# A slot-attention kernel: the key side in blocks of 64 tokens instead of 128

## The chip, the cores and the metric

The kernel runs on one core of a Trainium2 chip. The core has five engines that run side by side and wait for each other through semaphores: TensorE (PE, matrix products; PEld is its loading of weights), VectorE (DVE), ScalarE (ACT), GpSimd (POOL) and SyncE (SP, which here only starts transfers). TensorE writes its results into PSUM, which has eight banks of 128 partitions x 512 f32; DVE and ACT read them from there. The metric is the device time of one launch in microseconds, the lower the better.

## The reference

Four sequences of 512 tokens with 512 features go through one layer: a gated slot attention with 16 heads (keys of 64, values of 128, 64 slots), and a feed-forward part with rounded weights. The part that matters here is the recurrence of each head over time. In the notation of the reference:

```python
z = jax.lax.cumlogsumexp(s, axis=2)
g = jnp.exp(jnp.concatenate([z[:, :, :1], z[:, :, :-1]], axis=2) - z)
p = jnp.exp(s - z)
...
def step_k(hk, x):
    q_t, k_t, p_t, g_t = x
    hk = hk * g_t[:, :, None, :] + k_t[..., None] * p_t[:, :, None, :]
    return (hk, jnp.einsum('bhk,bhkm->bhm', q_t, hk))
_, okT = jax.lax.scan(step_k, hk0, (qT, kT, pT, gT))
pvT = jax.nn.softmax(okT, axis=-1)
```

With e = exp(s) and z turned into the running sum of e, the decay cancels: the score of token t for slot m is the sum over all tokens u up to t of (q_t . k_u) e_u[m], divided by the running sum of e[m] at t. That is a causal linear attention. It can be worked out in blocks of tokens: within a block by a masked product of queries and keys times e, and for all earlier blocks through a state, the sum of k_u e_u over their tokens (64 x 64 for each head). A second recurrence of the same form then carries the values; it stays as it is.

## The kernel before, in words

The attention is cut into 32 units, one for each pair of heads g (0 to 7) and sequence b (0 to 3). The order is g 0 to 7 for b 0 and 1 in turn, then the same for b 2 and 3. After the units comes the feed-forward part for the four sequences. The whole program is under a manual schedule: each engine runs its instructions in the order in which the code emits them, so the order of the calls in `attention` is the order of the work on every engine.

Two heads share a unit, each with 64 of the 128 partitions wherever a tile holds "slots" or "keys". A unit projects slots, keys and queries (`project`, L557), turns e and the keys so that tokens lie on partitions (`turn_e`, L697, `turn_k`, L702), projects the values (`project_v`, L570) and the gate (`gate_main`, L823, `gate_mixed`, L831), and takes the scores through a softmax to the values. The output of the unit before is finished in between: `turn_output` (L837: four transposes on PE, then a product on DVE at L842), `high_output` (L847, ACT), `split_output` (L850, DVE), `project_output` (L861), `add_output` (L882, which also starts a transfer from POOL's queue).

The key side, which is changed, uses blocks of 128 tokens, four to a sequence (NT = 4):

- `key_states` (L707) forms the three states that are needed after block 0, 1 and 2: `states` (L630) makes six f32 products of 128 tokens, 64 columns each, the two heads in the two column halves of the array, into one PSUM bank. `add_up` (L645) adds them up on DVE: one copy, two additions. POOL copies the sums into `sk_both` (L713), whose blocks are 128 x 128 with the two heads on the diagonal and zeros beside it, cleared once at the start (L136).
- `query_key` (L715) calls `diagonal_blocks` (L607): eight products of 64 x 128 with 128 columns, the heads in the two row halves of the array, into two banks of the pool "acc"; then two masking products on DVE (L626) with the triangle `tri`.
- `slot_scores` (L718) sums into one bank: three products of `sk_both` with the queries (128 x 128, L724), then eight of e with the masked blocks (128 x 64, heads in the column halves, L731). DVE multiplies the bank by the inverse running sum into okT (L739), and `softmax` (L741) starts by transposing okT on PE.

Where these stand differs with g. In units of even g the order is turn_e, turn_k, values(0), values(1), turn_output(0) and (1) each followed by its high_output, key_states, inverse, query_key, values(2), split_output(0), values(3). In units of odd g it is turn_e, turn_output(0), turn_k, turn_output(1), both high_outputs, query_key, key_states, both split_outputs, inverse. Then in both the gate, slot_scores, value_states, softmax and the output projection follow. For b of 2 and 3 DVE also rounds the feed-forward weights (`quantize`, L461) in between.

PSUM is shared out by hand: three banks are taken in turn by `bank` (L110), two belong to "acc", three to the projections ("proj"). A tile that takes a bank waits until the last reader of its previous tile is done. The banks in turn are used by the transposes, by the states of keys and values, and by the second call of `diagonal_blocks`:

```python
    def bank(name, n=None):
        if n is None:
            n = turn[0]
            turn[0] = (n + 1) % 3
        if n in held:
            held.pop(n)()
        return ps1.tile([P, 512], F32, tag=f"bank{n}", name=name)
```

SBUF tiles are shared by tags in the same way: "ok" holds the softmax, "sv" the value states, "kn" the turned keys and later okT, "a0" and "a1" the masked blocks of both sides.

Of the kernel before, what the change touches and what calls it, by code (L numbers as in the profile page):

```python
# [37 lines left out]
F32 = mybir.dt.float32  # L38
# [3 lines left out]
ALU = mybir.AluOpType  # L42
AX = mybir.AxisListType

P = 128
# [4 lines left out]
def kernel(  # L50
# [18 lines left out]
    nc = tc.nc  # L69

    B, T, D = x.shape
# [4 lines left out]
    NT = T // P  # L76
    KC = D // P
    HG = 2
    NG = H // HG
    HM = HG * M  # L80
# [6 lines left out]
    const = ctx.enter_context(tc.tile_pool(name="const", bufs=1))  # L87
    xpool = ctx.enter_context(tc.tile_pool(name="xpool", bufs=2))
    one = ctx.enter_context(tc.tile_pool(name="one", bufs=1))
# [3 lines left out]
    ps2 = ctx.enter_context(tc.tile_pool(name="ps2", bufs=2, space=bass.MemoryType.PSUM))  # L93
# [4 lines left out]
    turn = [0]  # L98
    held = {}
# [10 lines left out]
# [7 lines that stand above are left out]
# [5 lines left out]
    tri = const.tile([P, P], F32, tag="tri", name="tri")  # L122
# [10 lines left out]
    mhalf = const.tile([P, NH], F32, tag="mhalf", name="mhalf")  # L133
    nc.gpsimd.memset(mhalf, -0.5)

    sk_both = const.tile([P, NT - 1, HM], F32, tag="sk_both", name="sk_both")  # L136
    nc.gpsimd.memset(sk_both, 0.0)
    QMAX = 464.0

    NS = 2 * NFC + 1  # L140
# [29 lines left out]
    def other(count=None):  # L170
        for _ in range(count or pace[0]):
            if work:
                work.pop(0)[1]()
# [9 lines left out]
    def need(key):  # L183

        while any(name == key for name, _ in work):
            other(1)
# [4 lines left out]
    for g in range(NG):  # L191
# [3 lines left out]
        for nm in names:  # L195
            n = g if nm != "v" else 0 if g == 0 else (g + 1) // 2
# [96 lines left out]
    def next_step():  # L293
        if steps:
            steps.pop(0)()
# [310 lines left out]

    def diagonal_blocks(lT, rT, name):  # L607

        if name[0] == "a":
            pa = [ps2.tile([P, T], F32, tag="acc", name=f"ps_{name}_{h}") for h in range(HG)]  # L610
        else:
            pa = []
            for h in range(HG):
                if turn[0] in held:
                    turn[0] = (turn[0] + 1) % 3
                pa.append(bank(f"ps_{name}_{h}"))
        pa = [p.rearrange("p (n t) -> p n t", n=NT) for p in pa]
        for n in range(NT):
            cols = slice(n * P, (n + 1) * P)
            for h in range(HG):  # L620
                rows = slice(h * M, (h + 1) * M)
                nc.tensor.matmul(pa[h][:, n, :], lT[rows, cols], rT[rows, cols], start=True, stop=True)  # L622
        blocks = []
        for h in range(HG):
            a = one.tile([P, NT, P], F32, tag=f"a{h}", name=f"{name}_{h}")
            nc.vector.tensor_tensor(a, pa[h], tri.unsqueeze(1).to_broadcast([P, NT, P]), ALU.mult)  # L626
            blocks.append(a)
        return blocks

    def states(left, right, right0, width, name):  # L630


        pt = bank(name)[:, : (NT - 1) * width].rearrange("p (n w) -> p n w", w=width)
        for n in range(NT - 1):
            for h in range(HG):
                nc.tensor.matmul(
                    pt[h * M : (h + 1) * M, n, :],
                    left[:, n, h * M : (h + 1) * M],
                    right[:, n, right0 + h * width : right0 + (h + 1) * width],
                    start=True,  # L640
                    stop=True,
                )
        return pt

    def add_up(state, pt):  # L645

        nc.vector.tensor_copy(state[:, 0, :], pt[:, 0, :])
        for n in range(1, NT - 1):
            nc.vector.tensor_tensor(state[:, n, :], pt[:, n, :], state[:, n - 1, :], ALU.add)  # L649
# [3 lines left out]
    class Heads:  # L653
# [48 lines left out]
        def turn_k(self):  # L702
            pt = transpose_4(self.kT, f"ps_kn_{self.u}")
            self.kn = one.tile([P, NT, HM], F32, tag="kn", name=f"kn_{self.u}")
            nc.scalar.copy(self.kn, pt)

        def key_states(self):  # L707
            pt = states(self.kn, self.e, 0, M, f"ps_sk_{self.u}")
            self.sk = one.tile([P, NT - 1, M], F32, tag="sk", name=f"sk_{self.u}")
            add_up(self.sk, pt)  # L710
            for h in range(HG):
                rows = slice(h * M, (h + 1) * M)
                nc.gpsimd.tensor_copy(sk_both[rows, :, h * M : (h + 1) * M], self.sk[rows])  # L713

        def query_key(self):  # L715
            self.a = diagonal_blocks(self.kT, self.qT, f"a_{self.u}")

        def slot_scores(self):  # L718


            pok = ps2.tile([P, T], F32, tag="acc", name=f"ps_ok_{self.u}")
            for n in range(1, NT):
                cols = slice(n * P, (n + 1) * P)
                nc.tensor.matmul(  # L724
                    pok[:, cols], sk_both[:, n - 1, :], self.qT[:, cols],
                    start=(n == 1), stop=False,
                )
            for n in range(NT):
                for h in range(HG):
                    rows = slice(h * M, (h + 1) * M)  # L730
                    nc.tensor.matmul(  # L731
                        pok[rows, n * P : (n + 1) * P],
                        self.e[:, n, rows],
                        self.a[h][:, n, :],
                        start=False,
                        stop=(n == NT - 1),
                    )
            self.okT = one.tile([P, T], F32, tag="kn", name=f"okT_{self.u}")
            nc.vector.tensor_tensor(self.okT, pok, self.rzT, ALU.mult)  # L739

        def softmax(self):  # L741

# [147 lines left out]
    def first_unit():  # L890


        X = Heads(0, 0)

        parts = layernorm(0, 1, first=lambda: X.values(0))
        for nm in "skqv":
            load_matrix(nm, 0, True)
        for item in [item for item in work if item[0] in ("s_", "k_", "q_")]:
            work.remove(item)
            item[1]()  # L900
        X.values(1)
        for _ in range(5):
            piece()
        transposing = layernorm(1, 1)
        work.extend(parts())
        load_matrix("g", 0, True)
        other(2)
        X.slots()
        other(2)
        X.keys(X.running_sum)  # L910
        other(2)
        X.queries(None)
        X.turn_e()
        X.turn_k()
        other(2)
        X.values(2)
        other(2)
        X.key_states()
        X.inverse()
        X.values(3)  # L920
        fetch()
        fetch()
        load_matrix("o", 0, True)
        other(1)
        transposing()
        next_step()
        other(2)
        X.query_key()
        next_step()
        other(3)  # L930
        X.gate_main(0)
        X.slot_scores()
        X.value_states()
        next_step()
        X.softmax()
        X.softmax_exp()
        other(1)
        X.gate_main(1)
        X.slot_weights()
        next_step()  # L940
        X.gate_silu(0)
        X.gate_silu(1)
        exp_and_log()
        X.weight_slot()
        need("xs_1")
        X.softmax_sum()
        need("xs_0")
        piece()
        X.read_out()
        return X  # L950

    def attention(g, b, before, load, gated):
# [3 lines left out]
        X = Heads(g, b)  # L956
# [4 lines left out]
        def early_step():  # L961

            if not any(name.endswith("_m") for name, _ in work):
                next_step()

        need(f"xs_{b}")
        need("s")
        X.slots()
# [20 lines left out]
        if even:  # L989
            X.turn_k()  # L990
            next_step()
            if turned():
                other(1)
            need("v")
            X.values(0)
            if first or b > 1:
                other(1)
            X.values(1)
            before.turn_output(0)
            before.high_output(0)  # L1000
            before.turn_output(1)
            before.high_output(1)
            X.key_states()
            X.inverse()
            X.query_key()
            other()
            X.values(2)
            before.split_output(0)
            next_step()
            other()  # L1010
            X.values(3)
            other()
            next_step()
            before.split_output(1)
        else:
            before.turn_output(0)
            X.turn_k()
            before.turn_output(1)
            before.high_output(0)
            before.high_output(1)  # L1020
            X.query_key()
            X.key_states()
            if b > 1:
                early_step()
            before.split_output(0)
            before.split_output(1)
            X.inverse()
            if work and work[0][1] is scale_low:
                other(1)
            if work and work[0][0] == "o":  # L1030
                other()
# [153 lines left out]
    with tc.manual_schedule(engines=EVERY):  # L1185
# [83 lines left out]
        for b in range(B):  # L1269
            need(f"xs_{b}")  # L1270
            for c in range(NFC):
                if c > 1:
                    other(2)
                h = ffn_hidden(b, c)
# [74 lines left out]
```

## Time and profile before

| what | value |
|---|---|
| time, median of 3 runs | 1456.88 us (1455.47 to 1457.69) |
| span of the profiled execution | 1454.5 us (what lies around it isn't on the page; the median less the span is 2.4 us) |
| granted TensorE clock, mean | 0.999 |
| ps_sk, matmul passes (L636, N = 64) | x384, median 222 ns |
| ps_a (L622), ps_ok (L731), N = 128 | x512 each, median 272 and 273 ns |
| ps_ok (L724), N = 128 | x192, median 275 ns |
| masks of a on DVE (L626) | x64, median 680 ns |
| okT on DVE (L739) | x32, median 692 ns |
| sk copies on POOL (L713) | x64, mean 679 ns |

A matmul's duration in the trace runs from its start to its end, and the next ones start long before that: the distance between starts is what it costs the stream. The count of passes is twice the count of f32 matmuls in the code. In a timeline a line is a run of equal instructions: its start, the time from the first start to the last end, engine, line, operation, tiles, shape, count, and in brackets the idle time of the engine before it with what ended it. In the chain, pieces follow each other without overlap, so their lengths add up.

### The profile page before, as it was taken

How to read it: one execution, taken by the hardware profiler on the slowest of the kernel's cores; microseconds unless marked ns; L12 is line 12 of the kernel's file. 1: busy time of each engine (PE TensorE's matmuls, PEld its weight loads, DVE VectorE, ACT ScalarE, POOL GpSimd, SP SyncE). 2: the span in 40 equal slices, each digit the busy share in tenths (PEclk: the TensorE clock that was granted, in tenths of full speed). 3: DMA queues.
4: the chain of work that ended last, by engine and by line, in shares of the span. 5: the costliest groups of instructions: out<-in, count | busy, mean ns of one | idle time of the engine just before them, and what ended most of it. 6: DMA issues, size and time to landing. Idle time of an engine off the chain costs nothing.

```text
span 1454.5 us, 22772 instructions
## 1 busy us (share of the span) xinstructions
PE 1429.6 (98%) x8875; PEld 1178.9 (81%) x8875; DVE 1104.0 (76%) x1968; ACT 709.9 (49%) x1215; POOL 240.0 (16%) x271
## 2 busy tenths in 40 slices
PE   9999999999999999999999999999999999999998
PEld 4778888888888888888888888888888788888886
DVE  6888868976897689878888898898889863435333
ACT  4555555555665556554545554556445542222221
POOL 2012111211121122211211121111112111000000
PEclk9999999999999999999999999999999999999999
DMA  8274556565655474456546654666465562101000
GB/s 333 86 218 138 182 160 172 175 191 158 174 174 185 135 232 123 138 156 192 160 109 196 203 161 108 196 203 173 127 179 174 145 181 30 59 0 58 1 29 29
DMA packets 80859, 212.51 MB, mean 146 GB/s; under 512 B 6168, under 2 KB 35120, under 8 KB 75568
## 3 DMA queue, kind: packets, MB, share of 16 engines
q1 hardware_dynamic: 62224, 177.49, 33.1%
q0 software_dynamic: 18528, 33.58, 15.2%
q8 instruction: 70, 1.15, 0.3%
q14 instruction: 37, 0.30, 0.1%
HBM read 107.23 MB, written 108.00 MB: 148 GB/s over the span
## 4 chain that ended last, share of the span: by engine, by line
PE 89%; DVE 7%; ACT 2%; issue 1%; POOL 0%; DMA 0%; DVEq 0%; POOLq 0%
PE ps_o L869 8%; PE ps_g L528 8%; PE ps_v L587 7%; PE ps_fg L1097 6%; PE ps_fu L1097 6%; PE ps_ov L793 4%; PE ps_o_m L869 4%; PE ps_g_m L551 4%; PE ps_v_m L587 4%; PE ps_s L528 3%; PE ps_k L528 3%; PE ps_q L528 3%; PE ps_fd L1158 3%; PE ps_fe L1158 3%; PE ps_b L622 2%; PE ps_a L622 2%
## 5 line engine op out<-in xcount | busy, mean ns | idle before, releaser
L885 POOL DMA_DIRECT2D stream<-y x128 | 112.4, 884 | 476.3 <-DVE y L884 468.6
L869 PE MATMUL ps_o<-w_o,oT 128*128 128x512 f32 x512 | 145.2, 405 | 0.0
L528 PE MATMUL ps_g<-xs,w_g 128*128 128x512 f32 x496 | 125.2, 394 | 0.0
L587 PE MATMUL ps_v<-w_v,xs 128*128 128x512 f32 x480 | 122.3, 397 | 0.2 <-DVE qT L555 0.2
L1118 DVE SCALAR_TENSOR_TENSOR h<-ps_fu,scol,act 128x512 f32<-128x512 f32 x48 | 36.0, 750 | 111.5 <-PE ps_fu L1097 110.2
L879 ACT ACTIVATE y<-ps_o 128x512 f32<-128x512 f32 x128 | 76.5, 598 | 74.9 <-PE ps_o L869 74.9
L528 PEld LDWEIGHTS ps_g<-xs,w_g 128*128 128x128 f32 x496 | 91.7, 188 | 19.7
L869 PEld LDWEIGHTS ps_o<-w_o,oT 128*128 128x128 f32 x512 | 91.4, 188 | 17.4
L587 PEld LDWEIGHTS ps_v<-w_v,xs 128*128 128x128 f32 x480 | 87.7, 188 | 19.4 <-DVE qT L555 0.6
L713 POOL COPY sk_both<-sk 64x192 f32<-64x192 f32 x64 | 43.5, 679 | 343.4 <-DVE sk L649 341.5
L1097 PE MATMUL ps_fg<-xs,wf 128*128 128x512 f32 x384 | 95.6, 391 | 0.0
L884 DVE TENSOR_TENSOR y<-y,ps_o_m 128x512 f32<-128x512 f32 x128 | 87.2, 681 | 10.4 <-ACT y L879 9.8
L1097 PE MATMUL ps_fu<-xs,wf 128*128 128x512 f32 x384 | 94.8, 389 | 0.0
L595 ACT ACTIVATE v<-ps_v 128x512 f32<-128x512 f32 x60 | 35.9, 599 | 99.9 <-PE ps_v L587 99.9
L803 ACT ACTIVATE og<-ps_ov 128x512 f32<-128x512 f32 x64 | 38.1, 597 | 94.5 <-PE ps_ov L793 94.5
L1097 PEld LDWEIGHTS ps_fu<-xs,wf 128*128 128x128 f32 x384 | 72.1, 188 | 15.0
L1097 PEld LDWEIGHTS ps_fg<-xs,wf 128*128 128x128 f32 x384 | 71.6, 188 | 14.6
L869 PE MATMUL ps_o_m<-w_o,oT 128*128 128x512 f32 x256 | 79.4, 391 | 0.2 <-ACT y L879 0.2
L596 DVE TENSOR_TENSOR v<-v,ps_v_m 128x512 f32<-128x512 f32 x60 | 41.0, 684 | 48.6 <-PE ps_v_m L587 48.6
L1124 ACT CAST both<-h 128x512 fp32r<-128x512 f32 x48 | 29.8, 621 | 94.5 <-DVE h L1118 94.5
L1115 ACT ACTIVATE act<-ps_fg,scol 128x512 f32<-128x512 f32 x48 | 33.0, 688 | 87.7 <-PE ps_fg L1097 87.7
L533 ACT ACTIVATE sg<-ps_g 128x512 f32<-128x512 f32 x62 | 37.0, 596 | 71.4 <-PE ps_g L528 44.4
(171 smaller groups left out, 3327.0 us busy)
## 6 DMA issues: line engine op xcount, KB each, us to landing
stream<-y POOLq DMA_DIRECT2D x128, 256.0 KB, 6.3
split_v<-w_v SPq DMA_DIRECT2D x4, 3072.0 KB, 12.3
split_g<-w_g SPq DMA_DIRECT2D x8, 1536.0 KB, 7.6
split_o<-w_o SPq DMA_DIRECT2D x8, 1536.0 KB, 6.3
w_v<-split_v SPq DMA_DIRECT2D x4, 3072.0 KB, 16.3
w_g<-split_g SPq DMA_DIRECT2D x8, 1536.0 KB, 6.6
w_o<-split_o SPq DMA_DIRECT2D x8, 1536.0 KB, 9.5
rounded<-qw SPq DMA_DIRECT2D x36, 256.0 KB, 3.7
```

The costliest lines, as they stand in the source:

```text
L528: nc.tensor.matmul(self.p, products(self.nm, c, self.col0, i), xs[self.b][i][:, c, :], start=(i == 0 and c == 0), stop=(i == 1 and c == KC ...
L551: nc.tensor.matmul(self.m, products(self.nm, c, self.col0, 2), xs[self.b][2][:, c, :], start=(c == 0), stop=(c == KC - 1),)
L587: nc.tensor.matmul(dst, xs[b][i][:, c, n * P : (n + 1) * P], wt["v"][:, i, c * 2 * HV : (c + 1) * 2 * HV], start=(i == which[0] and c == 0 ...
L622: nc.tensor.matmul(pa[h][:, n, :], lT[rows, cols], rT[rows, cols], start=True, stop=True)
L713: nc.gpsimd.tensor_copy(sk_both[rows, :, h * M : (h + 1) * M], self.sk[rows])
L793: nc.tensor.matmul(po[h][:, n, :], self.bb[h][:, n, :], both_v[self.b][:, n, self.v0 + h * DV : self.v0 + (h + 1) * DV], start=False, stop ...
L869: nc.tensor.matmul(dst, self.oT[:, i, h, n * P : (n + 1) * P], wt["o"][:, i, h * D : (h + 1) * D], start=(i == which[0] and h == 0), stop= ...
L879: nc.scalar.mul(y, p, 1.0 + DELTA)
L884: nc.vector.tensor_tensor(y, y, m, ALU.subtract)
L885: nc.gpsimd.dma_start(stream[self.b][n * P : (n + 1) * P, :], y, accum_op=ALU.add)
L1097: nc.tensor.matmul(pp, w[:, c * P : (c + 1) * P], xs[b][k][:, c, :], start=(c == 0 and k == 0), stop=(c == KC - 1 and k == 1),)
L1158: nc.tensor.matmul(sums[n], parts[k][:, n * P : (n + 1) * P], fw[c][2], start=(c == 0 and k == 0), stop=(c == NFC - 1 and k == 1),)
```

## The change

Blocks of the key side become 64 tokens long, eight to a sequence (SB = 64). A block of 128 tokens now has two halves, "sub" 0 and 1.

- `key_states` makes 14 products of 64 x 64 with 64 columns: the half of the block picks the row half of the array, the head the column half. The two halves go to two banks taken in turn. ACT copies the first bank into a new tile "own" (tag "sv"), DVE adds the second bank to it and adds up over blocks (three operations), and POOL writes the sums into `sk_even` and, added to own, into `sk_odd` (six operations in all). `sk_odd` shares the tag "ok" with the softmax, so POOL clears it in every unit (`clear_odd`), at the unit's start.
- `query_key` makes 16 products of 64 x 64 with 64 columns: the head picks the row half, the half of the block the column half. The masks are 128 x 256 for each head.
- `slot_scores` sums into two banks of "acc", one for each half: 14 products of the seven states (128 x 64, 64 columns, head by head), and 16 of e with the masked blocks (64 x 64, 64 columns). okT is written by two DVE operations, one for each bank.
- In units of odd g key_states moves ahead of query_key.

```diff
-    sk_both = const.tile([P, NT - 1, HM], F32, tag="sk_both", name="sk_both")
-    nc.gpsimd.memset(sk_both, 0.0)
+    SB = P // 2
+    tri_sub = const.tile([P, SB], F32, tag="tri_sub", name="tri_sub")
+    for sub in range(2):
+        rows = slice(sub * SB, (sub + 1) * SB)
+        nc.gpsimd.tensor_copy(tri_sub[rows, :], tri[rows, rows])
+
+    sk_even = const.tile([P, NT - 1, HM], F32, tag="sk_even", name="sk_even")
+    nc.gpsimd.memset(sk_even, 0.0)
...
+        def clear_odd(self):
+
+            self.sk_odd = one.tile([P, NT, HM], F32, tag="ok", name=f"sk_odd_{self.u}")
+            nc.gpsimd.memset(self.sk_odd, 0.0)
+
         def key_states(self):
-            pt = states(self.kn, self.e, 0, M, f"ps_sk_{self.u}")
-            self.sk = one.tile([P, NT - 1, M], F32, tag="sk", name=f"sk_{self.u}")
-            add_up(self.sk, pt)
+
+            pts = [
+                bank(f"ps_sk_{self.u}_{sub}")[:, : NT * M].rearrange("p (n w) -> p n w", w=M)
+                for sub in range(2)
+            ]
+            for n in range(NT):
+                for sub in range(2):
+                    toks = slice(sub * SB, (sub + 1) * SB)
+                    for h in range(HG):
+                        if 2 * n + sub == 2 * NT - 1:
+                            continue
+                        cols = slice(h * M, (h + 1) * M)
+                        nc.tensor.matmul(
+                            pts[sub][cols, n, :], self.kn[toks, n, cols], self.e[toks, n, cols],
+                            start=True, stop=True,
+                        )
+            own = one.tile([P, NT, M], F32, tag="sv", name=f"sk_own_{self.u}")
+            nc.scalar.copy(own, pts[0])
+            sk = one.tile([P, NT - 1, M], F32, tag="sk", name=f"sk_{self.u}")
+            nc.vector.tensor_tensor(sk, pts[1][:, : NT - 1, :], own[:, : NT - 1, :], ALU.add)
+            for n in range(1, NT - 1):
+                nc.vector.tensor_tensor(sk[:, n, :], sk[:, n, :], sk[:, n - 1, :], ALU.add)
             for h in range(HG):
                 rows = slice(h * M, (h + 1) * M)
-                nc.gpsimd.tensor_copy(sk_both[rows, :, h * M : (h + 1) * M], self.sk[rows])
+                nc.gpsimd.tensor_copy(self.sk_odd[rows, 0, rows], own[rows, 0, :])
+            for h in range(HG):
+                rows = slice(h * M, (h + 1) * M)
+                nc.gpsimd.tensor_copy(sk_even[rows, :, rows], sk[rows])
+                nc.gpsimd.tensor_tensor(
+                    self.sk_odd[rows, 1:, rows], own[rows, 1:, :], sk[rows], ALU.add
+                )
 
         def query_key(self):
-            self.a = diagonal_blocks(self.kT, self.qT, f"a_{self.u}")
+
+            pa = [ps2.tile([P, T], F32, tag="acc", name=f"ps_a_{self.u}_{h}") for h in range(HG)]
+            pa = [p[:, : NT * SB].rearrange("p (n t) -> p n t", n=NT) for p in pa]
+            for n in range(NT):
+                for sub in range(2):
+                    c = slice((2 * n + sub) * SB, (2 * n + sub + 1) * SB)
+                    for h in range(HG):
+                        rows = slice(h * M, (h + 1) * M)
+                        nc.tensor.matmul(
+                            pa[h][sub * SB : (sub + 1) * SB, n, :], self.kT[rows, c], self.qT[rows, c],
+                            start=True, stop=True,
+                        )
+            self.a = []
+            for h in range(HG):
+                a = one.tile([P, NT, SB], F32, tag=f"a{h}", name=f"a_{self.u}_{h}")
+                nc.vector.tensor_tensor(
+                    a, pa[h], tri_sub.unsqueeze(1).to_broadcast([P, NT, SB]), ALU.mult
+                )
+                self.a.append(a)
 
         def slot_scores(self):
...
+            for c in range(1, 2 * NT):
+                n, sub = divmod(c, 2)
+                state = self.sk_odd[:, n, :] if sub else sk_even[:, n - 1, :]
+                for h in range(HG):
+                    cols = slice(h * M, (h + 1) * M)
+                    nc.tensor.matmul(
+                        pok[sub][cols, n, :], state[:, cols], self.qT[:, c * SB : (c + 1) * SB],
+                        start=(c <= 2), stop=False,
+                    )
             for n in range(NT):
-                for h in range(HG):
-                    rows = slice(h * M, (h + 1) * M)
-                    nc.tensor.matmul(
-                        pok[rows, n * P : (n + 1) * P],
-                        self.e[:, n, rows],
-                        self.a[h][:, n, :],
-                        start=False,
-                        stop=(n == NT - 1),
-                    )
+                for sub in range(2):
+                    toks = slice(sub * SB, (sub + 1) * SB)
+                    for h in range(HG):
+                        cols = slice(h * M, (h + 1) * M)
+                        nc.tensor.matmul(
+                            pok[sub][cols, n, :], self.e[toks, n, cols], self.a[h][toks, n, :],
+                            start=False, stop=(n == NT - 1),
+                        )
             self.okT = one.tile([P, T], F32, tag="kn", name=f"okT_{self.u}")
-            nc.vector.tensor_tensor(self.okT, pok, self.rzT, ALU.mult)
+            okT, rzT = (t.rearrange("p (n s t) -> p n s t", s=2, t=SB) for t in (self.okT, self.rzT))
+            for sub in range(2):
+                nc.vector.tensor_tensor(okT[:, :, sub, :], pok[sub], rzT[:, :, sub, :], ALU.mult)
...
             before.high_output(0)
             before.high_output(1)
+            X.key_states()
             X.query_key()
-            X.key_states()
```

`clear_odd` is called at the start of each unit, ahead of the projection of the slots.

More of the change, by code (lines that the diff above doesn't have):

```diff
@@ L607, in diagonal_blocks @@
     def diagonal_blocks(lT, rT, name):
[L609 to L612, printed above, removed]
-            for h in range(HG):
-                if turn[0] in held:
-                    turn[0] = (turn[0] + 1) % 3
-                pa.append(bank(f"ps_{name}_{h}"))
+        pa = []
+        for h in range(HG):
+            if turn[0] in held:
+                turn[0] = (turn[0] + 1) % 3
+            pa.append(bank(f"ps_{name}_{h}"))
         pa = [p.rearrange("p (n t) -> p n t", n=NT) for p in pa]
@@ L711, in key_states @@
             for h in range(HG):
                 rows = slice(h * M, (h + 1) * M)
-                nc.gpsimd.tensor_copy(sk_both[rows, :, h * M : (h + 1) * M], self.sk[rows])
-        def query_key(self):
-            self.a = diagonal_blocks(self.kT, self.qT, f"a_{self.u}")
-        def slot_scores(self):
[L721 to L726, printed above, removed]
-                )
-            for n in range(NT):
-                for h in range(HG):
-                    rows = slice(h * M, (h + 1) * M)
-                    nc.tensor.matmul(
-                        pok[rows, n * P : (n + 1) * P],
-                        self.e[:, n, rows],
-                        self.a[h][:, n, :],
-                        start=False,
-                        stop=(n == NT - 1),
-                    )
+                nc.gpsimd.tensor_copy(self.sk_odd[rows, 0, rows], own[rows, 0, :])
@@ new lines, in slot_scores @@
+        def slot_scores(self):
+            pok = [
+                ps2.tile([P, T], F32, tag="acc", name=f"ps_ok_{self.u}_{sub}") for sub in range(2)
+            ]
+            pok = [p[:, : NT * SB].rearrange("p (n t) -> p n t", n=NT) for p in pok]
+            for c in range(1, 2 * NT):
[7 more added lines that the diff above has]
+                    )
+            for n in range(NT):
+                for sub in range(2):
+                    toks = slice(sub * SB, (sub + 1) * SB)
+                    for h in range(HG):
+                        cols = slice(h * M, (h + 1) * M)
[3 more added lines that the diff above has]
+                        )
@@ L900, in first_unit @@
             item[1]()
+        X.clear_odd()
         X.values(1)
@@ L964, in early_step @@
                 next_step()
+        X.clear_odd()
         need(f"xs_{b}")
```

## The prediction

> **What bounds the kernel now.** I read the page first: busy times and the chain that ended last.
>
> ```profile
> PE 1429.6 (98%) x8875; PEld 1178.9 (81%) x8875; DVE 1104.0 (76%) x1968; ACT 709.9 (49%) x1215; POOL 240.0 (16%) x271
> PE 89%; DVE 7%; ACT 2%; issue 1%; POOL 0%; DMA 0%; DVEq 0%; POOLq 0%
> ```
>
> TensorE sets the end for 89% of the span, DVE for 7%. So an edit counts twice: what it takes from TensorE's stream, and what it does to DVE where TensorE waits for it. Second, the chain in order of time, through unit (0,2):
>
> ```profile
> 611.01 0.87 PE ps_oT L604 x8
> 611.88 0.50 PE ps_sk L636 x12
> 612.38 1.09 PE ps_a L622 x16
> 613.47 2.04 PE ps_v L587 x8
> ...
> 626.07 0.67 PE ps_ok L724 x6
> 626.74 1.05 PE ps_ok L731 x16
> 627.78 0.02 issue
> 627.81 0.70 DVE okT L739
> 628.51 0.04 issue
> 628.55 0.66 PE ps_okn L604 x4
> ```
>
> Each f32 matmul shows as two passes (6 matmuls of sk are x12). The touched work is 0.50 + 1.09 + 0.67 + 1.05 = 3.3 us of a unit, 106 us over 32 units; behind it TensorE stands until DVE has written okT. Third, the timelines of DVE and ACT, in even unit (2,2), then in odd unit (1,2):
>
> ```profile
> 756.86 1.40 DVE L842 SCALAR_TENSOR_TENSOR sg<-ps_oT,scol,sg 128x512 f32<-128x512 f32 x2
> 758.18 0.21 DVE L647 COPY sk<-ps_sk 128x64 f32<-128x64 f32 x1
> 757.64 1.29 ACT L848 ACTIVATE oT<-sg 128x512 fp32r<-128x512 f32 x2 [1.76 <-DVE sg L842]
> 771.47 0.69 DVE L739 TENSOR_TENSOR okT<-ps_ok,rzT 128x512 f32<-128x512 f32 x1 [0.57 <-PE ps_ok L731]
> ```
> ```profile
> 690.36 0.58 ACT L705 COPY kn<-ps_kn 128x512 f32<-128x512 f32 x1 [0.29 <-PE ps_kn L604]
> 690.71 1.16 PE L622 MATMUL ps_a<-qT,kT 64*128 64x128 f32 x16
> 693.11 0.21 DVE L647 COPY sk<-ps_sk 128x64 f32<-128x64 f32 x1
> 699.83 0.69 DVE L739 TENSOR_TENSOR okT<-ps_ok,rzT 128x512 f32<-128x512 f32 x1 [0.63 <-PE ps_ok L731]
> ```
>
> DVE is about 0.6 us early for okT. In most units it runs from sk to there without a gap, so a delay of DVE above 0.6 us near sk reaches TensorE.
>
> **Prices on TensorE.** From the matmul start times of the trace: sk starts two passes, one in each column half, every 0.058 us (64 columns); a and the e·a products of ok start two every 0.109 to 0.111 (128 columns). A change of tile shape adds 0.093 before the first pass; the first slot of 64 wide passes is 0.048 longer than the later ones.
>
> The unknown is a slot with four 64x64 tiles. One end is 0.058 (all four run together), the other 0.116 (two at a time, as seen). I take 0.058: near 558 us the two row halves of ps_b ran 23 ns out of step, each at its own 0.111, and ps_ov started in one half before ps_b's last pass in the other. Halves are thus fed independently.
> [...]
>
> **Key side, per unit.** Before: span of sk 0.347, change 0.152, a 0.890, change 0.202: 1.591 us from sk's start to the next group. After: sk is 14 matmuls, at most 8 slots a tile, 0.048 + 7 x 0.058 = 0.454; a follows in the same shape, 0.058 + 0.42 (0.406 and 0.014 for the tiles' stagger); change 0.151. Sum 1.083: **-0.508**. Then two new waits.
> Even g: sk now takes two banks, and of the three in turn the second is that of turn_output(0), which DVE's first L842 frees at 0.66 after sk's start in every even unit. Only the first pair of products goes ahead; sk ends 1.05 instead of 0.454 after its start: +0.60, net **+0.09**. Queued behind the waiting matmul: the rest of sk, a, values(2).
> Odd g: key_states moves ahead of query_key, so the copy of kn (ends at 690.94; a started at 690.71) is no longer covered by a's matmuls: +0.30, net **-0.21**.
>
> **Scores.** From the last gate matmul to okn it was 0.233 + 0.557 + 0.205 + 0.822 + 1.069 = 2.886. After: 0.320 (the shape changes here too), 14 state products, two at a time, 0.802; change 0.151; e·a 0.468. The last pass is 0.05 shorter, so okT could start 0.126 earlier. But okT is now two operations of 256: between 291 ns (128) and 692 (512) I get 0.425, with 0.08 overlap 0.77 instead of 0.69: +0.08. The change of shape into sv (0.146) hides under okT.
>
> **DVE, ACT, POOL.** The first DVE operation of sk waits for a new ACT copy "own", which is queued behind both L848. In (2,2) these end 1.98 after sk's start, own (256 columns: between 374 and 600 ns, say 0.44) at 2.44. DVE's sum starts at 2.49 and hands over at 3.28 (0.79 for three operations instead of 0.65); before it was 1.88: 1.40 late. The masks of a shrink from 2 x 0.61 to 2 x 0.345, -0.53: **0.87 late** from then on. Queued behind: inverse, split_output, the value and gate subtractions, okT. Odd g, by the same count from a's start (L848 ends at 1.52, own at 2.0, next 3.53 instead of 3.05): **0.48 late**.
> POOL has six operations where it had two copies of 0.68, and a memset (0.41 for 384 columns, some 0.55; POOL idles many us before it). A row for 64x192 additions is missing; between 0.68 and 1.28 (128x512). In odd g the chain ends 5.8 to 7.0 after a's start, scores begin at 7.0: hidden, just. Where POOL's copies ran beside DVE, L852 took 0.826 instead of 0.684: 0.14 for two copies. With four more operations I take 2 x 0.14, +0.3 on DVE; the ends are 0 (the copies beside other operations cost nothing) and 4 x 0.14, 0.56.
> [...]
>
> **Sum at okn.** TensorE offers okT -0.34 (odd) or -0.04 (even); DVE offers it at lateness minus idle minus 0.08; the later counts, plus 0.08.
> - Odd, 13 units with idle about 0.61: 0.78 - 0.69 = +0.09, so +0.17 each, 2.2. Units (1,1), (7,1) have no idle: +0.85 each, 1.7. (7,3) has a gap of 1.63: -0.26.
> - Even, b below 2: gaps of DVE swallow the 1.17; +0.04 x 7 = 0.3. b of 2 and 3: idle 0.57 twice gives +0.60, 0.83 three times +0.34, the rest +0.04: 2.3.
> - (0,0), without the two waits: -0.3.
>
> Together +5.9 us. The span 1454.5 + 5.9, and 2.4 around it (median 1456.88 less the span): **1462.8**. The feed-forward part (from 1180 us) is untouched.
>
> **Rivals.**
> 1. *Four tiles don't run four at a time*, so the change does not do what it says. [...] At 0.116: +1.13 and +1.43, 41 us: 1498. For it: no four tiles in this trace. Against: the independent halves. 0.24.
> 2. *Not slower: DVE's idle covers the late sum.* Place: the gap before okT. If lateness stays under some 0.3 in odd and 0.6 in even units (own faster, no POOL cost), TensorE's times count: 16 x (-0.26) + 16 x 0.04 = -3.5, 1453. If sk's second bank is also free at once, 15 x 0.6 = 9 more: 1444. For it: the 0.6 us gaps, and DVE loses 0.2 us of work a unit. Against: ACT's order is fixed, with L848 ahead of own. It decides from the point where okT still shows idle time before it in odd units. About 1449; 0.20.
> 3. *The forecast*: TensorE saves, and the bank, kn, own and POOL take it back. 0.56; own range 1453 to 1472.
>
> **From these.** Predicted 1463. Below 1450 lies about half of rival 2, above 1488 about a third of rival 1, so the range is 1450 to 1488. A measurement tells 0.2% (2.9 us) from no change. Faster than 1454: 0.17 of rival 2 and 0.08 of the forecast, 0.25. Within: 0.03 and 0.12, 0.15. Slower: 0.60.
>
> **What would show it.** Right: ps_a and the e·a products about 0.45 us each; a wait of sk for DVE's L842 in even units, for kn in odd ones; DVE idle over 1 us before sk's first operation, on ACT; no idle before okT in odd units. Wrong: ps_a still 0.9 us (rival 1); idle before okT (rival 2); TensorE waiting for POOL at the state products, which I count as hidden.

## The result, and the profile after

The changed kernel takes 1470.87 us (median of 4 runs, 1468.55 to 1473.83) against 1456.24 us before: a ratio of 1.0103, 95% interval 1.0091 to 1.0114. Slower, as forecast, and inside the range, but by 14.6 us where 6 were forecast. The profiled execution, the fastest of the four, has a span of 1466.8 us, 12.3 more than before; the sums below are made against that.

The page first, busy times and the chain by engine:

```profile
PE 1423.1 (97%) x11115; PEld 1157.5 (79%) x11115; DVE 1114.2 (76%) x2000; ACT 715.0 (49%) x1247; POOL 317.8 (22%) x433
PE 73%; DVE 19%; ACT 4%; issue 3%; DMA 1%; POOL 0%; SPq 0%; DVEq 0%; POOLq 0%; ACTq 0%
```

TensorE has 2240 more matmul passes and is busy for 6.5 us less: the blocks of 64 do save. But its share of the chain has fallen from 89% to 73%, and DVE's has risen from 7% to 19%. The end is now set by DVE in stretches where it was set by TensorE. Where, the waits of the changed kernel show (in all us, times, longest). Lines have moved: L900 was L842 (turn_output), L910 L852 (split_output), L602 L596 (the value subtraction), L797 L739 (okT); L733 is the new copy own.

```profile
DVE sk L735 <- ACT sk_own L733: 29.7, 31, 1.0
PEld ps_okn L610 <- DVE okT L797: 18.2, 32, 2.0
PEld ps_sk L728 <- ACT kn L708: 8.1, 16, 0.9
PEld ps_sk L728 <- DVE sg L900: 7.7, 15, 0.5
PEld ps_g L534 <- DVE v L602: 7.6, 15, 0.7
```

Before, TensorE had the second of these waits too, but shorter:

```profile
PEld ps_okn L604 <- DVE okT L739: 13.3, 32, 1.0
```

Its other three are new. TensorE's products of sk wait for kn in 16 units (odd g) and for the bank of the first turned output in 15 (even g): both were forecast. The last was not priced: the gate's first matmuls wait for a value subtraction on DVE, 15 times in 11 even units. The first line is new as well, and a source of that lateness: DVE stands 1 us in nearly every unit until ACT has copied own.

Even unit (2,2) on TensorE's timeline, then the same unit in the chain in order of time:

```profile
764.19 0.33 PE L728 MATMUL ps_sk<-e,kn 64*64 64x64 f32 x4
764.90 0.58 PE L728 MATMUL ps_sk<-e,kn 64*64 64x64 f32 x24 [0.38 <-DVE sg L900]
765.29 0.65 PE L757 MATMUL ps_a<-qT,kT 64*64 64x64 f32 x32
...
778.37 0.69 PE L790 MATMUL ps_ok<-a,e 64*64 64x64 f32 x32
```
```profile
764.18 1.33 DVE sg L900 x2
765.51 0.02 issue
765.53 0.63 ACT oT L906
766.16 0.27 ACT sk_own L733
...
766.46 0.37 DVE sk L735
...
770.99 0.69 DVE v L602
771.68 0.04 issue
771.72 2.12 PE ps_g L534 x8
```

The first four passes of sk go at 764.19, the other 24 at 764.90, when DVE's first L900 has freed the bank. Then 32 passes of a, four array tiles side by side, take 0.65 us from first start to last end; 16 passes took 1.16 before. The chain shows what sets the end: high_output on ACT, own behind it, the sum on DVE, and down DVE's queue to the value subtraction, at whose end the gate starts. Before, in the same unit, the gate started when TensorE got there, 0.74 us after that subtraction had ended:

```profile
762.70 0.68 DVE L596 TENSOR_TENSOR v<-v,ps_v_m 128x512 f32<-128x512 f32 x1
764.12 1.98 PE L528 MATMUL ps_g<-xs,w_g 128*128 128x512 f32 x8
```

Odd unit (1,2), in the chain:

```profile
698.12 0.63 ACT oT L906
698.75 0.27 ACT sk_own L733
699.02 0.02 issue
699.04 0.37 DVE sk L735
...
702.27 1.02 DVE oT L910
...
706.53 0.68 DVE okT L797 x2
707.21 0.04 issue
707.25 0.66 PE ps_okn L610 x4
```

Here the chain of DVE runs through to okT without a gap. L910 takes 1.02 us in it, and 0.68 when nothing is in its way: GpSimd's writes of the states run beside it.

### The profile page after: what moved, and what is told of

It reads as the page before. It is cut to its first block, busy times and chain, and to the rows that moved or that the text cites. A ratio compares the mean times of both kernels' runs of the same rounds, so it can differ in the third digit from the quotient of the medians.

```text
span 1466.8 us, 27585 instructions
## 1 busy us (share of the span) xinstructions
PE 1423.1 (97%) x11115; PEld 1157.5 (79%) x11115; DVE 1114.2 (76%) x2000; ACT 715.0 (49%) x1247; POOL 317.8 (22%) x433
## 3 DMA queue, kind: packets, MB, share of 16 engines
q8 instruction: 87, 1.43, 0.4%
## 4 chain that ended last, share of the span: by engine, by line
PE 73%; DVE 19%; ACT 4%; issue 3%; DMA 1%; POOL 0%; SPq 0%; DVEq 0%; POOLq 0%; ACTq 0%
PE ps_o L927 8%; PE ps_fg L1157 6%; PE ps_fu L1157 6%; PE ps_v L593 5%; PE ps_g L534 4%; PE ps_o_m L927 4%; PE ps_ov L851 4%; PE ps_s L534 3%; PE ps_q L534 3%; PE ps_k L534 3%; PE ps_fd L1218 3%; PE ps_fe L1218 3%; PE ps_v_m L593 3%; PE ps_b L625 2%; DVE sg L900 2%
## 5 line engine op out<-in xcount | busy, mean ns | idle before, releaser
L927 PEld LDWEIGHTS ps_o<-w_o,oT 128*128 128x128 f32 x512 | 91.5, 188 | 17.5
L740 POOL COPY sk_odd<-sk_own 64x64 f32<-64x64 f32 x64 | 16.1, 252 | 313.7 <-ACT sk_own L733 311.8
L1157 PEld LDWEIGHTS ps_fg<-xs,wf 128*128 128x128 f32 x384 | 71.6, 188 | 14.6
L866 POOL TENSOR_TENSOR rs<-rs,mhalf 128x8 f32<-128x8 f32 x32 | 58.4, 1824 | 77.9 <-DVE rs L863 50.0
```

The costliest lines, as they stand in the source:

```text
L866: nc.gpsimd.tensor_tensor(rs, rs, mhalf.rearrange("p (h n) -> p h n", h=HG), ALU.pow)
L927: nc.tensor.matmul(dst, self.oT[:, i, h, n * P : (n + 1) * P], wt["o"][:, i, h * D : (h + 1) * D], start=(i == which[0] and h == 0), stop= ...
L1157: nc.tensor.matmul(pp, w[:, c * P : (c + 1) * P], xs[b][k][:, c, :], start=(c == 0 and k == 0), stop=(c == KC - 1 and k == 1),)
```

## The experiments

Three theories are set against each other. Theory A says that queue order is the cause: TensorE saves what was computed, and DVE's lateness, from own's place on ACT and a little from GpSimd, is what TensorE waits for. Theory B puts the lateness on GpSimd's work. Theory C says that four tiles and the changes of shape cost more than they save. All times are compared with runs of the kernel before on the same chip, whose medians were 1456.09 (first four) and 1455.85 (last four).

**e1_own_first.** key_states ahead of the high_outputs, in both kinds of units; the cut shows the even ones:

```diff
-            before.high_output(0)
             before.turn_output(1)
-            before.high_output(1)
             X.key_states()
+            before.high_output(0)
+            before.high_output(1)
```

> Theory A (queue order): DVE is late because the ACT copy own stands behind both high_outputs, and the lateness reaches TensorE in two places: the first gate matmul of even units (its bank waits for a late value subtraction, about 6 us in all) and okT in odd units (about 0.5 us in each of 16). Issuing key_states ahead of the high_outputs brings own some 0.5 to 0.7 us forward, so both go: 1457 to 1461, and the wait of the gate for DVE shrinks from 7.6 us to under 2. The waits of sk for its second bank and for kn stay. Theory B (GpSimd blocks DVE): nothing moves by more than 3 us, 1468 to 1472. Theory C (the array itself: four tiles and the changes of shape cost more than they save): no change, 1469 to 1473.

Measured: 1459.04, ratio to the kernel before 1.0023 (1.0014 to 1.0033). Of the 14.6 us, 12 are gone by an exchange on ACT's queue alone. The waits:

```profile
DVE sk L735 <- ACT sk_own L733: 15.9, 31, 0.6
PEld ps_okn L610 <- DVE okT L797: 12.8, 32, 1.7
PEld ps_sk L728 <- ACT kn L708: 8.0, 16, 0.9
PEld ps_sk L728 <- DVE sg L900: 7.7, 15, 0.5
PEld ps_g L534 <- DVE v L602: 1.8, 4, 0.6
```

DVE waits half as long for own; the gate waits 4 times instead of 15. The two waits of sk stand unchanged, as they should. Theory C falls, and B can't be the whole of it.

**e2_no_pool.** The six GpSimd writes of a unit are left out:

```diff
-                nc.gpsimd.tensor_copy(self.sk_odd[rows, 0, rows], own[rows, 0, :])
...
-                nc.gpsimd.tensor_copy(sk_even[rows, :, rows], sk[rows])
-                nc.gpsimd.tensor_tensor(
-                    self.sk_odd[rows, 1:, rows], own[rows, 1:, :], sk[rows], ALU.add
-                )
```

> Leaves out the six GpSimd writes of the states per unit, so the contribution of earlier blocks to the scores is missing. Theory A: DVE is late by 0.3 us less, of some 1.0 (even) and 0.8 (odd): 5 to 8 us off, 1463 to 1466, and own is still waited for about 1 us in each unit. Theory B: nearly all of the loss over the kernel before goes, 1456 to 1459, and the gate no longer waits for DVE. Theory C: no change.

Measured: 1456.81, ratio 1.0004 (0.9995 to 1.0014). That is theory B's number: 14 us, twice what A allowed. The groups of DVE show the means, in the changed kernel and then without the writes (one row each: line, operation, shape, count, total and mean ns):

```profile
L910 DVE TENSOR_TENSOR oT<-sg,oT 128x512 fp32r<-128x512 f32 x64 | 54.0, 844 | 1.4 <-ACT oT L906 1.4
```
```profile
L901 DVE TENSOR_TENSOR oT<-sg,oT 128x512 fp32r<-128x512 f32 x64 | 43.7, 682 | 1.4 <-ACT oT L897 1.4
```

And the busy times of the page without the writes:

```profile
PE 1419.6 (98%) x11115; PEld 1159.5 (80%) x11115; DVE 1097.7 (76%) x2000; ACT 716.1 (49%) x1247; POOL 214.3 (15%) x241
```

DVE's busy time falls from 1114.2 to 1097.7 us, with the same 2000 instructions: GpSimd stretches it by 16.5 us, 0.52 in each of 32 units. Yet DVE still waited 29.7 us for own, as A had it. So both are at work, and A had GpSimd's part, 0.3 us a unit, at little more than half its size.

**e3_bank.** The second bank of sk comes from the projections' pool, so it is free at once:

```diff
             pts = [
-                bank(f"ps_sk_{self.u}_{sub}")[:, : NT * M].rearrange("p (n w) -> p n w", w=M)
-                for sub in range(2)
+                bank(f"ps_sk_{self.u}_0"),
+                ps3.tile([P, T], F32, tag="proj", name=f"ps_sk_{self.u}_1"),
             ]
+            pts = [p[:, : NT * M].rearrange("p (n w) -> p n w", w=M) for p in pts]
```

> The second bank of sk comes from the projections' pool, where it is free at once. Theory A: the 0.6 us wait at sk goes in 15 even units (9 us), but DVE is as late as it was in absolute time, so in the some 10 units where the gate waits for DVE that wait grows by about as much: only 2 to 5 us net, 1466 to 1469, and the gate's wait for DVE rises from 7.6 to 12 us or more. If the bank were simply additive: 1462. Theory C: the bank's wait is a symptom and nothing changes.

Measured: 1467.08, ratio 1.0077 (1.006 to 1.0094): 4 us off, not 9. The wait moved (the file is a line longer here, so L736 is L735 of the changed kernel):

```profile
DVE sk L736 <- ACT sk_own L734: 29.7, 31, 1.0
PEld ps_okn L610 <- DVE okT L798: 18.2, 32, 2.0
PEld ps_g L534 <- DVE v L602: 12.1, 13, 1.3
```

TensorE reaches the gate 0.6 us earlier in even units and, in 11 of the 15, waits there for a DVE that is no earlier. By the start times the four others, (2,1), (4,1), (6,1) and (0,2), keep the 0.6 us.

**e4_order.** The same arithmetic in another order; even units first, then odd ones:

```diff
             before.turn_output(0)
-            before.high_output(0)
-            before.turn_output(1)
-            before.high_output(1)
             X.key_states()
-            X.inverse()
             X.query_key()
+            before.turn_output(1)
+            before.high_output(0)
+            before.high_output(1)
+            X.inverse()
...
             before.turn_output(1)
+            X.query_key()
+            X.key_states()
             before.high_output(0)
             before.high_output(1)
-            X.key_states()
-            X.query_key()
```

> Same arithmetic, other order: even units turn_output(0), key_states, query_key, turn_output(1), then the high_outputs; odd units query_key ahead of key_states, high_outputs last. No bank is waited for, kn is covered by a, own is not behind the high_outputs. Theory A: TensorE's own saving of 0.51 + 0.05 us a unit comes through in most units, 1438 to 1447, faster than the kernel before. Theory B: GpSimd's work still makes DVE late, 1454 to 1460. Theory C: 1460 or more.

Measured: 1441.82, ratio 0.9905 (0.9891 to 0.992), faster than the kernel before by 14 us. Its chain in even unit (0,2):

```profile
604.17 0.44 PE ps_oT L610 x4
604.61 0.55 PE ps_sk L728 x26
605.16 0.05 PE ps_a L757 x2
605.22 0.47 PE ps_a L757 x30
605.68 0.65 PE ps_oT L610 x4
606.34 1.86 PE ps_v L593 x8
```

It stays on TensorE from the transposes to the values; sk and a together take 1.07 us of it, 1.59 before. By the start times, the way from turn_e to the scores is 0.30 to 0.46 us shorter than before in 20 of the 32 units, and that from the scores to okn 0.12 to 0.15 shorter in nearly all. Not everything is gained: (1,1) and (7,1) still lose 0.6 us between scores and okn, and (7,3) loses 1.6 ahead of its scores.

**e5_before_order.** The kernel before, blocks of 128, with the edit of e4_order.

> The kernel before, blocks of 128, in the order that made the changed kernel fast. If that order is worth something by itself, it would be faster here too, down to 1442 to 1450, and the 64-token blocks would be worth nothing. Theory A (the blocks save TensorE time, the order only removes waits that the change had brought): the kernel before had none of these waits, so 1454 to 1458, no change.

Measured: 1455.55, ratio 0.9997 (0.9988 to 1.0006). The order is worth nothing without the small blocks; in this order it is the blocks that save 14 us.

**e6_order_no_pool** has the edits of e4_order and e2_no_pool together.

> The reordered kernel without the six GpSimd writes per unit (the earlier blocks' contribution to the scores is missing). Theory A, lateness only counts above DVE's idle time: in the new order DVE has little lateness left, so the same 0.4 to 0.5 us of GpSimd's blocking that cost 14 us before now costs 1 to 4: 1438 to 1441. If GpSimd's cost were a fixed sum per unit: 14 us again, 1428.

Measured: 1439.78, ratio 0.9892 (0.9878 to 0.9907): 2 us less than e4_order. DVE's busy time falls by 17.5 us here too (1116.2 to 1098.7): the same stretching, of which nearly all is now inside idle time.

**e7_own_first_no_pool** has the edits of e1_own_first and e2_no_pool.

> key_states ahead of the high_outputs and no GpSimd writes (the earlier blocks' contribution is missing): both sources of DVE's lateness away, the waits of sk for its bank and for kn stay. Theory A: they overlap, since either alone brings DVE nearly inside its idle time; TensorE's own times then count, odd units -0.33, even units +0.03 us: 1449 to 1453. If the two were additive (12 and 14 us): 1445 or less.

Measured: 1454.01, ratio 0.9989 (0.998 to 0.9999): 17 us under the changed kernel, where the two alone gave 12 and 14. They overlap, as expected, though the time is 1 us above the range given. Part of that is unit (7,3): between its products of sk and its scores stand the transposes of a layernorm that wait for DVE, and by the start times the unit loses 1.9 us instead of gaining.

**e8_odd_only** reorders odd units as e4_order does and leaves even ones as changed.

> Only odd units reordered (query_key ahead of key_states, both ahead of the high_outputs); even units as in the changed kernel. Theory A: odd units lose 6.9 us in the changed kernel and gain 4.6 in the reordered one, so 11 to 12 us off: 1458 to 1461; the wait of sk for kn is gone, that for its second bank and the gate's wait for DVE stay at some 15 and 8 us. If odd and even units influence each other, it differs by more than 3 us.

Measured: 1457.63, ratio 1.0015 (1.0006 to 1.0025), just under the range. The wait for kn is gone from its list, and the two of even units stand:

```profile
PEld ps_g L534 <- DVE v L602: 8.0, 15, 0.7
PEld ps_sk L728 <- DVE sg L900: 7.7, 15, 0.5
```

So the losses of odd and even units are nearly separate. By the start times, from one turn_e to the next, the even units lose 7.1 us here (6.9 in the changed kernel) and the odd ones gain 4.1 (4.6 in e4_order; in the changed kernel they lose 6.9). By the medians the odd order is worth some 13 us and, from this run to e4_order, the even one 16; by the traces 11 and 14.

## Why the forecast was right in sign and wrong in size

- **Prices on TensorE: right.** Four tiles run together. a's 32 passes start within 0.43 us in even units (0.42 forecast), the state products span 0.81 (0.80), e·a 0.48 (0.47). Rival 1 is out: its 1498 is for slots of 0.116 us, two tiles at a time, which by its sum would make okn 1.13 us later in odd units and 1.43 in even ones. Four passes share 0.058 us. The upper end of the range, 1488 with about a third of rival 1 above it, leaves room for a price between the two as well, and no run shows one: in the changed kernel e·a's slots of four passes follow each other, after the first, 0.058 to 0.059 us apart in all 32 units.
- **The two new waits of sk: right.** sk spans 1.07 us in even units (1.05 forecast); in odd units it starts about 0.29 late (0.30). e8_odd_only and e4_order take them out one after the other.
- **Scores to okn: right.** From the first state product to okn the forecast came to 2.52 us, against 2.65 before: 0.13 less. In even units, where DVE is in time for okT, it is 0.146 less.
- **DVE's lateness: near in size.** In (2,2) the value subtraction starts 6.80 us after sk's start, 5.75 before: 1.05 late, 1.17 forecast (0.87 and 0.3). That the sum came so near is partly luck, for its parts were off in opposite ways. own takes 0.354 us, not 0.44, and ends 2.23 us after sk's start, not 2.44: in (2,2) its place makes 0.65 of the 1.05, and two operations beside GpSimd's writes make the other 0.40.
- **GpSimd on DVE: mis-sized.** The forecast took "2 x 0.14, +0.3 on DVE" for four more operations. Six operations stretch DVE by 0.52 us a unit (e2_no_pool). Both sides are slowed: L910, with two SBUF inputs, takes 844 ns in the mean with the writes and 682 without, and in (1,2) GpSimd's copy of 64x192 takes 0.34 us beside a mask of a and 0.72 beside L910. The masks, which read PSUM and SBUF, run beside the writes in 62 of 64 cases and take 406 to 420 ns in all 64. Why L910 is slowed and the masks are not, no run here shows.
- **The step that failed: the sum at okn.** I named the value and gate subtractions as queued behind the late sum, and then let only okT count: "Even, b below 2: gaps of DVE swallow the 1.17". But the value subtraction comes before those gaps, and it frees a projection bank. In (2,2) before, it ended at 763.38 and the gate's matmul started at 764.12: a slack of 0.74, less than the lateness. The gate's weight loads waited so 15 times, and after such a pause the group of eight matmuls takes 2.10 to 2.14 us instead of 1.98. By the start times, from one turn_e to the next, even units lost 6.9 us (without (0,0)), where I had 2.6. The 11 units in which the gate waits lost 6.6 of it up to okn; the four others lost 0.03 each, as forecast (0.04). In none of the 15 did TensorE reach okT too early, since it had already waited at the gate.
- **Odd units: the right place, a little more of it.** Units (1,1) and (7,1), without idle time, lost 1.2 and 1.3 (0.85 each forecast; by the forecast's own rule it should have read 0.78). (7,3) lost 0.9 where a gain of 0.26 stood, since there TensorE goes on to transposes that wait for DVE. The other 13 lost 3.5 in all (2.2): ten lost 0.10 to 0.20 each up to okn, where 0.17 was forecast, but (1,3), (3,2) and (5,0) lost 0.43 to 0.53. In these three the first transposes of the turned output also wait 0.25 to 0.34 us for the copy of e on ACT, which no term had.
- **The balance.** Even units +6.9, odd units +6.9, (0,0) -0.35 (-0.3 forecast), and -1.1 at the start of the program: in the trace before, the first eight matmuls of the values took 6.10 us, in that after 4.83, ahead of any changed product. Together 12.3, the difference of the spans. The trace of e5_before_order, with blocks of 128, also starts 0.7 us sooner than that before, so the 1.1 is not to be read as a gain of the change.
- **Rival 2 was the version not tried.** Its condition, DVE early enough at okT and sk's second bank free at once, is what e4_order sets up (1441.82, 1444 priced); ACT's fixed order spoke against it, and that order can be changed.

## What to carry to other kernels

When an engine becomes late, follow its queue instruction by instruction and ask of each which buffer it frees and how much slack that buffer's next user has: the smallest slack on the way decides, not the last wait. A saving on the busiest engine is worth only what the order on the other queues lets through; here one and the same arithmetic is 1% slower or 1% faster. Costs below the slack all but vanish and costs above it count: GpSimd's writes were worth 14 us in one order and 2 in the other. So remove such costs together before judging any one of them.

## What the runs showed of the hardware

The tiles of the array need not keep step: in odd unit (1,2) of the changed kernel two passes of a start at 697.92, before the last two of sk at 697.97. By the code it is the row half with two products of sk fewer that goes ahead; the trace doesn't name the tile. A second effect was unexpected: in the even unit above, the same eight 512-wide matmuls of the gate take 0.14 us longer when they start after a pause of the weight loads. It is the same 2.1 that the values took before, after the change of tile shape from a (2.11 us). Why both cost the same, no run here shows.
